# A sequence in the Mamba stage as two blocks of 128 steps, with a state handed from the first to the second

## The chip, the cores and the metric

The kernel runs on one core of a Trainium2 chip. The metric is the device time of one launch in microseconds (us). The time before is the median of three runs.

## What is computed

The reference is a chain of four residual layers over 4096 tokens of 128 features (16 sequences of 256 steps), each ahead of it a layer norm: a latent attention, six layers of local attention with a feed-forward, a Mamba layer (state-space scan), and two more layers of local attention with a feed-forward. The change touches only the Mamba layer. Its core in the reference, cut to what matters (four heads of 64 channels, a state of 64):

```python
X = x * dt[..., None]
Adt = A * dt
...
A_cumsum = jnp.cumsum(Ac, axis=-1)
Lmat = jnp.exp(segsum(Ac))                       # exp(sum of A*dt over j < k <= i), 0 above the diagonal
Y_diag = jnp.einsum('bclhn,bcshn,bhcls,bcshp->bclhp', Cc, Bc, Lmat, Xc)
decay_states = jnp.exp(A_cumsum[..., -1:] - A_cumsum)
states = jnp.einsum('bclhn,bhcl,bclhp->bchpn', Bc, decay_states, Xc)
...
state_decay_out = jnp.exp(A_cumsum)
Y_off = jnp.einsum('bclhn,bchpn,bhcl->bclhp', Cc, states, state_decay_out)
Y = (Y_diag + Y_off).reshape(b, L, NHEADS, HEADDIM) + x * D[:, None]
y = Y.reshape(b, L, D_INNER)
y = y * jax.nn.silu(z)
y = y * jax.lax.rsqrt(jnp.mean(y * y, axis=-1, keepdims=True) + EPS) * norm_w
return jnp.einsum('bld,ed->ble', y, out_proj_w)
```

The length of the chunks is free: any split of the sequence gives the same result, as long as the state at a chunk's start carries what came earlier. Each sequence starts from `init_states`.

## The kernel before

Activations are kept with the 128 features on the partitions. Between the layers, x lies in DRAM (`xd`), 512 tokens (two sequences) to a tile, eight tiles in all. The Mamba stage (`mamba`) has two kinds of work, written as generators that are advanced in turn; here no order is written out by hand, a scheduler orders the instructions of each engine from what they depend on and from its own costs. The attention layers before and after it do have an order by hand (`PLAN32`, `PLAN64`) and are not touched.

`project(t)` takes a tile of 512 tokens: `normed` (center on TensorE at L149, mean of squares at L157, `var` on VectorE at L161, `rstd` as a power on GpSimd at L116, its spread over the partitions at L167), then the step sizes `dt` and `a` = A*dt (L1375, `softplus`), the convolution's three groups of channels (L1385 with four VectorE taps each, L1388 and L1393, and a Silu on ScalarE) and the gate `sz` (L1411).

`scan(b)` takes one sequence of 256 steps. It uses PSUM pools of two banks each (`s`, `mm`, `o`; `t` is the projection's):

- `pc` (pool `s`): C times B for the pairs of steps, blocks (0,0), (0,1) and (1,1) of 128x128, 384 columns; `cbm` on VectorE multiplies by the triangle `tri` of three blocks.
- `xdt`: x turned by four transposes (L1451), times dt.
- For each of two groups c of two heads: `ab` copies on GpSimd, running sums of `a` by matmuls with `tri` (L1469, L1470), their exp `ce` times C (L1473). For each head: weights `w0`, `w1` on VectorE (L1479, L1480), three matmuls for the segment sums of the three blocks (L1482, L1483, L1486), exp on ScalarE (L1488), product with `cbm` on GpSimd (L1489). Then `py` (pool `o`): the initial state times `ce` (L1493), and for each head and block of earlier steps a matmul of 64 columns (L1497).
- `y2`: plus D*x (L1504), times the gate (L1507), squares `sq` on GpSimd (L1509), their mean (L1515), `var` (L1519), `rstd` (L116), its spread (L1525), the scaling (L1530), the output projection (L1533), and the addition to x (L1534).

`leave(t)` stores the tile and norms it once more for the next attention layers (`norm_to_y`, whose two VectorE products are L180). Two sequences are in flight at a time, and the next tile's projection and the last tile's `leave` are advanced between their steps. On SP the stage issues eight loads (L1351) and eight stores (L1538, L1580).

TensorE's f32 matmul appears in the trace as two passes, so its counts are twice the calls; transposes have one.

Of the kernel before, what the change touches and what calls it, by code (L numbers as in the profile page):

```python
# [22 lines left out]
F32 = mybir.dt.float32  # L23
BF16 = mybir.dt.bfloat16
I32 = mybir.dt.int32
AF = mybir.ActivationFunctionType
ALU = mybir.AluOpType
AX = mybir.AxisListType

P = 128  # L30
B = 16
S = 256
# [1269 lines left out]
def mamba(ctx: ExitStack, k: Stack, m: Scan, last, later):  # L1302
# [9 lines left out]

    nc = k.nc
    H, DI, NC = 4, 256, 3
    TAPS = 4
# [1 line left out]
    work = ctx.enter_context(k.tc.tile_pool(name="mb_work", bufs=2))  # L1319
    deep = ctx.enter_context(k.tc.tile_pool(name="mb_deep", bufs=4))  # L1320


    tri = once.tile([P, 3, P], F32, name="tri")
    nc.gpsimd.memset(tri, 1.0)
    for i in (0, 2):
        nc.gpsimd.affine_select(
            out=tri[:, i, :],
            in_=tri[:, i, :],
            compare_op=ALU.is_ge,
            fill=0.0,  # L1330
            base=0,
            pattern=[[1, P]],
            channel_multiplier=-1,
        )
    tri = tri.rearrange("p c l -> p (c l)")
    gt = once.tile([P, P], F32, name="gt")
    nc.gpsimd.memset(gt, 1.0)
    nc.gpsimd.affine_select(
# [1 line left out]
    )  # L1340
    mean_w = once.tile([P, 1], F32, name="mb_mean_w")
    nc.gpsimd.memset(mean_w, 1.0 / DI)

    xs = {}

# [88 lines left out]
    def scan(b):  # L1434
# [3 lines left out]
        sl = slice(i0 * S, (i0 + 1) * S)  # L1438
        toks = [slice(i0 * S + i * P, i0 * S + (i + 1) * P) for i in range(2)]

        pc = k.ps("s")
        nc.tensor.matmul(pc[:, 0:S], bT[:, toks[0]], cT[0:E, sl], start=True, stop=True)
        nc.tensor.matmul(pc[:, S : 3 * P], bT[:, toks[1]], cT[0:E, toks[1]], start=True, stop=True)
        cbm = work.tile([P, 3 * P], F32, tag="cbm", name=k.name("cbm"))
        nc.vector.tensor_mul(cbm, tri, pc[:, 0 : 3 * P])
        xdt = work.tile([P, 2, H, E], F32, tag="xdt", name=k.name("xdt"))
        pt = k.ps("mm")
        for i in range(2):
# [5 lines left out]
            pt.rearrange("p (i h e) -> p i h e", i=2, e=E),  # L1454
            dt[:, 2 * i0 : 2 * i0 + 2, :].unsqueeze(3).to_broadcast([P, 2, H, E]),
        )
        yield
        y2 = work.tile([P, 2, S], F32, tag="y2", name=k.name("y2"))
        sqs = []
        for c in range(2):  # L1460
            pcs = k.ps("mm")[:, 0:S]
            sums = []
            for i in range(2):
                ab = deep.tile([P, 2, E], F32, tag=f"ab{i}", name=k.name("ab"))
                nc.gpsimd.tensor_copy(
                    ab, a[:, 2 * i0 + i, 2 * c : 2 * c + 2].unsqueeze(2).to_broadcast([P, 2, E])
                )
                sums.append(ab.rearrange("p h e -> p (h e)"))
            nc.tensor.matmul(pcs, sums[0], tri[:, 0:S], start=True, stop=False)  # L1469
            nc.tensor.matmul(pcs[:, P:S], sums[1], tri[:, 0:P], start=False, stop=True)  # L1470
            ce = work.tile([P, S], F32, tag="ce", name=k.name("ce"))
            nc.scalar.activation(ce, pcs, AF.Exp)
            nc.gpsimd.tensor_mul(ce, ce, cT[:, sl])  # L1473
            gs = []
            for h in (2 * c, 2 * c + 1):
                a0, a1 = (a[:, 2 * i0 + j, h : h + 1] for j in range(2))
                w0 = deep.tile([P, P], F32, tag="w0", name=k.name("w0"))
                w1 = deep.tile([P, P], F32, tag="w1", name=k.name("w1"))
                nc.vector.tensor_scalar_mul(w0, gt, a0)  # L1479
                nc.vector.tensor_scalar_mul(w1, gt, a1)  # L1480
                pseg = k.ps("s")
                nc.tensor.matmul(pseg[:, 0:S], w0, tri[:, 0:S], start=True, stop=False)  # L1482
                nc.tensor.matmul(  # L1483
                    pseg[:, P:S], a1.to_broadcast([P, P]), tri[:, 0:P], start=False, stop=True
                )
                nc.tensor.matmul(pseg[:, S : 3 * P], w1, tri[:, 0:P], start=True, stop=True)  # L1486
                g = deep.tile([P, 3 * P], F32, tag="g", name=k.name("g"))
                nc.scalar.activation(g, pseg[:, 0 : 3 * P], AF.Exp)  # L1488
                nc.gpsimd.tensor_mul(g, g, cbm)  # L1489
                gs.append(g)  # L1490
                yield
            py = k.ps("o")[:, 0:S]
            nc.tensor.matmul(py, initT[:, c, :], ce, start=True, stop=False)  # L1493
            for j in range(2):
                for i in range(2):
                    rows = slice(64 * i, 64 * i + 64)
                    nc.tensor.matmul(  # L1497
                        py[rows, j * P : S],
                        xdt[:, j, 2 * c + i, :],
                        gs[i][:, j * S : S + j * P],  # L1500
                        start=False,
                        stop=(j == 1),
                    )
            nc.vector.scalar_tensor_tensor(  # L1504
                y2[:, c, :], xc[:, c, sl], dcol[:, c : c + 1], py, ALU.mult, ALU.add
            )
            nc.vector.tensor_mul(y2[:, c, :], y2[:, c, :], sz[:, c, sl])  # L1507
            sq = deep.tile([P, S], F32, tag="sq", name=k.name("sq"))
            nc.gpsimd.tensor_mul(sq, y2[:, c, :], y2[:, c, :])  # L1509
            sqs.append(sq)  # L1510
            yield
# [162 lines left out]
```

## Time and profile before

| | us |
|---|---|
| median of 3 runs (4847.5 to 4858.25) | 4850.86 |
| the profiled execution, its own time | 4845.01 |
| its span | 4843.3 |
| Mamba stage in it, from its first memset (L1324) to its last addition's end (L1534) | 3745.7 to 4079.3 |
| one pair of sequences in that stage | 37.1 |

The page lists per engine the busy share of 40 equal slices of the span, a row with the granted TensorE clock in tenths, the chain of work that ended last, and groups of instructions by line with their count, busy time, mean and the idle time before them. A group's idle time names what ended it. Windows give the same busy times for a stretch between two times. A line can be that of a helper: L149 to L180 are called from `project` and from `leave`.

### The profile page before, as it was taken

The page shows a single profiled execution, that of the slowest core. Times are in us where ns is not written, and L with a number is a line of the kernel's source. Part 1 is how long each engine was busy: PE and PEld are TensorE (multiplying, and loading weights), DVE is VectorE, ACT ScalarE, POOL GpSimd, SP SyncE. Part 2 cuts the span into 40 slices and gives each one's busy share as a digit, 9 for nine tenths or more (in the row PEclk, how much of TensorE's full clock was granted, in tenths as well). Part 3 has the DMA queues.
Part 4 walks back from the last instruction along what each step waited for, and adds up shares of the span by engine and source line. Part 5 has one row for each costly group of instructions (what it writes and reads, how often), then busy time and mean ns, then how long its engine had stood idle before and what let it go on. Part 6 is the DMA issues. An engine that isn't in the chain of part 4 may idle for free.

```text
span 4843.3 us, 121149 instructions
## 1 busy us (share of the span) xinstructions
PE 4570.3 (94%) x50834; PEld 3051.0 (63%) x50834; DVE 3371.2 (70%) x4050; ACT 2745.0 (57%) x3412; POOL 3297.2 (68%) x3603
## 2 busy tenths in 40 slices
PE   7986899999999999999999999999998898999998
PEld 4553566666666666666666666666665665566664
DVE  4664777777777777777777777777773675788775
ACT  2553465666656666566655666556664453565554
POOL 2434677777777777777777777777774344777774
PEclk9998999999999999999999999999999898999999
DMA  1111010000100010001000010000011000111111
GB/s 32 36 32 45 16 39 16 16 16 18 39 16 21 16 41 16 16 16 39 17 16 16 16 39 17 16 16 23 23 26 30 25 12 18 55 45 44 49 57 39
DMA packets 208040, 131.52 MB, mean 27 GB/s; under 512 B 61261, under 2 KB 179417, under 8 KB 207497
## 3 DMA queue, kind: packets, MB, share of 16 engines
q1 hardware_dynamic: 197096, 118.78, 9.9%
q8 instruction: 403, 6.60, 0.6%
q0 software_dynamic: 8704, 4.48, 0.5%
q14 instruction: 141, 1.15, 0.1%
q10 hardware_dynamic: 1696, 0.51, 0.0%
HBM read 29.65 MB, written 8.39 MB: 8 GB/s over the span
## 4 chain that ended last, share of the span: by engine, by line
PE 71%; DVE 16%; POOL 5%; ACT 4%; issue 2%; SPq 1%; DMA 0%; DVEq 0%; ACTq 0%; POOLq 0%
PE py L1107 13%; PE pq L792 7%; PE hid L1164 6%; PE u L1081 6%; PE pk L792 5%; PE scores L994 5%; PE tq L882 4%; DVE n L849 3%; PE tp L1040 3%; PE fy L1198 3%; PE tk L882 2%; DVE rotq L817 2%; PE st L383 2%; POOL rstd L116 1%; DVE rotk L817 1%
## 5 line engine op out<-in xcount | busy, mean ns | idle before, releaser
L1107 PE MATMUL py<-oT,wvo 128*128 128x256 f32 x3072 | 679.0, 379 | 1.2 <-ACT oT L1094 1.2
L1034 POOL TENSOR_TENSOR pr<-pr,rs 128x1024 f32<-128x1024 f32 x256 | 489.5, 1912 | 275.5 <-DVE rs L1029 234.1
L853 POOL TENSOR_TENSOR rotq<-rotq,t2q 128x1024 f32<-128x1024 f32 x256 | 605.0, 2363 | 36.3 <-DMA w<-in_L_ffn_W 23.8
L1107 PEld LDWEIGHTS py<-oT,wvo 128*128 128x128 f32 x3072 | 576.4, 190 | 75.8 <-ACT oT L1094 1.6
L1094 ACT COPY oT<-u 128x1024 f32<-128x1024 f32 x384 | 377.0, 1015 | 316.0 <-PE u L1081 307.7
L792 PE MATMUL pq<-wqkv,y 128*128 128x512 f32 x1024 | 493.2, 605 | 25.8 <-DMA wqkv<-in_L_ffn_Wqkv 14.1
L873 POOL TENSOR_TENSOR rotq<-rotq,rn 128x1024 f32<-128x1024 f32 x256 | 488.9, 1910 | 11.2
L101 DVE TENSOR_TENSOR y<-y,py 64x256 f32<-64x256 f32 x256 | 107.2, 419 | 525.1 <-PE py L1107 523.4
L817 DVE TENSOR_TENSOR rotq<-pq,tab 128x1024 f32<-128x1024 f32 x256 | 313.3, 1224 | 220.6 <-ACT sqq L803 150.2
L899 ACT COPY qT<-tq 128x1024 f32<-128x1024 f32 (+1 forms) x256 | 230.7, 901 | 412.1 <-PE tq L882 412.1
L853 POOL TENSOR_TENSOR rotk<-rotk,t2k 128x1024 f32<-128x1024 f32 x192 | 453.9, 2364 | 0.0
L994 PEld LDWEIGHTS scores<-kT,qT 64*32 64x32 f32 (+1 forms) x26624 | 322.0, 108 | 160.2 <-issue 97.2
L1025 DVE TENSOR_REDUCE rs<-pr 128x16 f32<-128x1024 f32 (+1 forms) x256 | 312.3, 1220 | 156.7 <-ACT pr L1018 152.0
L803 ACT ACTIVATE sqq<-pq 128x1024 f32<-128x1024 f32 x256 | 261.9, 1023 | 263.3 <-PE pq L792 245.4
L1081 PE MATMUL u<-prT,vc 64*128 64x256 f32 x3072 | 404.4, 394 | 2.1 <-DVE t2k L829 0.3
L994 PE MATMUL scores<-kT,qT 64*32 64x64 f32 (+2 forms) x26624 | 400.6, 225 | 4.7 <-ACT kT L899 2.8
L792 PE MATMUL pk<-wqkv,y 128*128 128x512 f32 x768 | 393.4, 601 | 0.0
L1164 PE MATMUL hid<-fxn,w 128*128 128x512 f32 (+1 forms) x768 | 387.1, 615 | 4.8 <-DVE ga L1186 2.7
L862 POOL TENSOR_SCALAR rn<-n 128x64 int32<-128x64 int32 (+1 forms) x128 | 30.3, 236 | 518.7 <-DVE n L849 518.7
L873 POOL TENSOR_TENSOR rotk<-rotk,rn 128x1024 f32<-128x1024 f32 x192 | 365.3, 1903 | 0.1
L1018 ACT ACTIVATE pr<-pr 128x1024 f32<-128x1024 f32 x256 | 270.6, 1057 | 134.9 <-DVE pr L1010 125.2
L1005 DVE TENSOR_REDUCE nm<-scores 128x16 f32<-128x1024 f32 (+1 forms) x256 | 311.5, 1217 | 21.9 <-PE scores L994 21.0
(285 smaller groups left out, 9773.1 us busy)
## 6 DMA issues: line engine op xcount, KB each, us to landing
vc<-vt SPq DMA_DIRECT2D x1152, 32.0 KB
vc<-vt SPq DMA_DIRECT2D x64, 256.0 KB
vc<-vt SPq DMA_DIRECT2D x96, 128.0 KB
vc<-vt SPq DMA_DIRECT2D x576, 16.0 KB
wqkv<-in_L_ffn_Wqkv SPq DMA_DIRECT2D x12, 512.0 KB
x<-xd SPq DMA_DIRECT2D x23, 256.0 KB
xd<-x SPq DMA_DIRECT2D x22, 256.0 KB
wo<-in_L_ffn_Wo SPq DMA_DIRECT2D x6, 512.0 KB
```

The costliest lines, as they stand in the source:

```text
L792: self.nc.tensor.matmul(pq[:, 512 * int(half) : 512 * int(half) + 512], self.k.y[:, b, c0 : c0 + P], L.wqkv[:, col : col + 512], start=Tru ...
L817: self.nc.vector.tensor_mul(rot.rearrange("p (w h) e -> p w h e", w=ways), self.get(n, "p" + group).rearrange("p (w h e) -> p w h e", w=wa ...
L853: self.nc.gpsimd.tensor_add(rot, rot, self.done(n, "t2" + group))
L873: self.nc.gpsimd.tensor_mul(rot, rot, rn.unsqueeze(2).to_broadcast(list(rot.shape)))
L994: self.nc.tensor.matmul(sc[ch * W : (ch + 1) * W, par, c, first : self.KS], qT[rows, c, ch * W : (ch + 1) * W], kT[rows, c, t0 - W + first ...
L1005: self.nc.vector.tensor_reduce(nm, self.get(n, "scores"), AX.X, ALU.max, negate=True)
L1025: self.nc.vector.tensor_reduce(rs, self.by_head(n), AX.X, ALU.add)
L1034: self.nc.gpsimd.tensor_mul(pr, pr, rs)
L1081: self.nc.tensor.matmul(pu[:, par, :, j, :], self.vc[n % 3][rows, ch, :], prT[rows, :, ch * W : (ch + 1) * W], start=True, stop=True,)
L1094: self.nc.scalar.copy(self.get(n - blk, "oT")[:, :, q0 : q0 + 64].rearrange("p (c i) q -> p i c q", i=2), self.done(n, "u" + half).rearran ...
L1107: self.nc.tensor.matmul(py, w[:, c, :], oT[:, c, :], start=(c == 0), stop=(c == last))
L1164: self.nc.tensor.matmul(pg[0:n, at : at + TT], L.w1[:, col : col + n], self.get(t, "fxn"), start=True, stop=True,)
```

## The change

A sequence becomes two blocks of 128 steps. Inside a block everything is as before; the block (0,1), which joined early steps with late ones, is gone, and in its place the state at the end of the first block is formed and used for the second. In detail:

- `tri` is one triangle of 128x128, not three blocks.
- `pc` holds two blocks of C times B, and beside them B turned for the first block (L1451 of the new file) and the sum of `a` from each step to the block's end (L1452); ScalarE copies the first to `bs` and takes the exp of the second, `ea`; GpSimd forms `xa`, the first block's `xdt` times `ea` (L1475).
- The running sums restart in the second block, two matmuls of 128 columns (L1486). Their exp is kept as `decay`, for the state's update, beside `ce`.
- Segment sums of both heads and both blocks: one VectorE product for the weights (`seg`, L1499), four matmuls of 128 columns into one bank (L1510), one exp (L1514) and one product (L1515) of 512 columns.
- The state: two matmuls of 64x64 into a bank of pool `o` (L1521), each followed on VectorE by the initial state times the block's decay plus that product (L1524). Four state tiles take turns; they are zeroed once.
- The output: for each block the state at its start times `ce` (L1536), then the two heads' matmuls (L1538).

L1545, L1548, L1550, L1556, L1560, L1566, L1571, L1574 and L1575 of the new file are L1504, L1507, L1509, L1515, L1519, L1525, L1530, L1533 and L1534 of the old one.

```diff
-    tri = once.tile([P, 3, P], F32, name="tri")
+    tri = once.tile([P, P], F32, name="tri")
...
+    states = [once.tile([P, P], F32, name=f"state{i}") for i in range(4)]
+    for state in states:
+        nc.gpsimd.memset(state, 0.0)
...
         pc = k.ps("s")
-        nc.tensor.matmul(pc[:, 0:S], bT[:, toks[0]], cT[0:E, sl], start=True, stop=True)
-        nc.tensor.matmul(pc[:, S : 3 * P], bT[:, toks[1]], cT[0:E, toks[1]], start=True, stop=True)
-        cbm = work.tile([P, 3 * P], F32, tag="cbm", name=k.name("cbm"))
-        nc.vector.tensor_mul(cbm, tri, pc[:, 0 : 3 * P])
+        for i in range(2):
+            nc.tensor.matmul(
+                pc[:, bass.ts(i, P)], bT[:, toks[i]], cT[0:E, toks[i]], start=True, stop=True
+            )
+        nc.tensor.transpose(pc[:, S : S + E], bT[:, toks[0]], k.ident[0:E, 0:E])
+        nc.tensor.matmul(pc[:, S + E : S + E + H], gt, a[:, 2 * i0, :], start=True, stop=True)
+        cbm = work.tile([P, 2, P], F32, tag="cbm", name=k.name("cbm"))
...
+        bs = work.tile([P, E], F32, tag="bs", name=k.name("bs"))
+        nc.scalar.copy(bs, pc[:, S : S + E])
+        ea = work.tile([P, H], F32, tag="ea", name=k.name("ea"))
+        nc.scalar.activation(ea, pc[:, S + E : S + E + H], AF.Exp)
...
+        xa = work.tile([P, H, E], F32, tag="xa", name=k.name("xa"))
+        nc.gpsimd.tensor_mul(xa, xdt[:, 0], ea.unsqueeze(2).to_broadcast([P, H, E]))
...
-            nc.tensor.matmul(pcs, sums[0], tri[:, 0:S], start=True, stop=False)
-            nc.tensor.matmul(pcs[:, P:S], sums[1], tri[:, 0:P], start=False, stop=True)
+                nc.tensor.matmul(
+                    pcs[:, bass.ts(i, P)],
+                    ab.rearrange("p h e -> p (h e)"),
+                    tri,
+                    start=True,
+                    stop=True,
+                )
+            decay = work.tile([P, S], F32, tag="decay", name=k.name("decay"))
+            nc.scalar.activation(decay, pcs, AF.Exp)
             ce = work.tile([P, S], F32, tag="ce", name=k.name("ce"))
-            nc.scalar.activation(ce, pcs, AF.Exp)
-            nc.gpsimd.tensor_mul(ce, ce, cT[:, sl])
...
-                nc.vector.tensor_scalar_mul(w0, gt, a0)
-                nc.vector.tensor_scalar_mul(w1, gt, a1)
-                pseg = k.ps("s")
-                nc.tensor.matmul(pseg[:, 0:S], w0, tri[:, 0:S], start=True, stop=False)
+            nc.gpsimd.tensor_mul(ce, decay, cT[:, sl])
+            seg = deep.tile([P, 2, 2, P], F32, tag="w", name=k.name("w"))
+            nc.vector.tensor_mul(
+                seg,
+                gt.unsqueeze(1).unsqueeze(1).to_broadcast([P, 2, 2, P]),
...
+            pseg = k.ps("s")
+            for h in range(2):
+                for i in range(2):
+                    nc.tensor.matmul(
+                        pseg[:, bass.ts(2 * h + i, P)], seg[:, h, i], tri, start=True, stop=True
+                    )
+            g = deep.tile([P, 2, 2, P], F32, tag="g", name=k.name("g"))
+            nc.scalar.activation(g.rearrange("p h i l -> p (h i l)"), pseg, AF.Exp)
+            nc.gpsimd.tensor_mul(g, g, cbm.unsqueeze(1).to_broadcast([P, 2, 2, P]))
+            yield
+            pst = k.ps("o")
+            state = states[(2 * b + c) % 4]
+            for h in range(2):
+                rows = slice(64 * h, 64 * h + 64)
                 nc.tensor.matmul(
-                    pseg[:, P:S], a1.to_broadcast([P, P]), tri[:, 0:P], start=False, stop=True
+                    pst[rows, 64 * h : 64 * h + 64], bs, xa[:, 2 * c + h], start=True, stop=True
                 )
-                nc.tensor.matmul(pseg[:, S : 3 * P], w1, tri[:, 0:P], start=True, stop=True)
-                g = deep.tile([P, 3 * P], F32, tag="g", name=k.name("g"))
...
+                nc.vector.scalar_tensor_tensor(
+                    state[rows, rows],
+                    initT[rows, c, rows],
+                    decay[rows, P - 1 : P],
+                    pst[rows, rows],
+                    ALU.mult,
+                    ALU.add,
+                )
+            yield
             py = k.ps("o")[:, 0:S]
-            nc.tensor.matmul(py, initT[:, c, :], ce, start=True, stop=False)
-            for j in range(2):
-                for i in range(2):
-                    rows = slice(64 * i, 64 * i + 64)
+            for i, of in enumerate((initT[:, c, :], state)):
+                cols = bass.ts(i, P)
+                nc.tensor.matmul(py[:, cols], of, ce[:, cols], start=True, stop=False)
+                for h in range(2):
                     nc.tensor.matmul(
...
```

## The prediction

> **What bounds the kernel now.** I read the slices of the page first, to find the stage that the change touches, then windows of that stage, its groups by form, its chain of waits, and the timeline of TensorE.
>
> ```profile
> PE   7986899999999999999999999999998898999998
> ...
> PEclk9998999999999999999999999999999898999999
> ```
>
> The Mamba stage lies in slices 31 to 34: its first memset (L1324) starts at 3745.7 us, its last addition (L1534) at 4078.9. Everything the diff edits lies there, 333 us or 6.9% of the span, so no edit can move the total by more than a few per cent. Windows, first of the stage before and then of one pair of sequences in Mamba:
>
> ```profile
> 3550.00:3600.00 50.00, 49.30 (x620) 35.32 (x619) 35.09 (x38) 28.33 (x32) 36.54 (x43) 1.00 0.11 27
> ...
> 3861.40:3898.50 37.10, 34.26 (x195) 25.19 (x194) 26.34 (x72) 21.24 (x31) 18.95 (x28) 0.95 0.05 15
> 3898.50:3935.70 37.20, 34.71 (x195) 25.34 (x194) 26.63 (x73) 21.22 (x31) 18.94 (x28) 0.95 0.05 15
> ```
>
> Columns: length, then busy PE, PEld, DVE, ACT, POOL, then the granted clock. A pair of sequences repeats every 37.1 us. TensorE is busy for 34.5 of them, VectorE 26.5, ScalarE 21.2, GpSimd 18.9; the clock is 0.95, where the earlier stage has 1.00. So TensorE leads, but not alone: something makes it pause and lose clock. The chain of waits shows the pause, once per pair (start, length, what):
>
> ```profile
> 3912.26 0.57 PE o L1497 x2
> 3912.83 0.63 PE mm L1469 x2
> ...
> 3914.94 0.17 DVE var L161
> ...
> 3915.18 1.02 POOL rstd L116
> ...
> 3919.51 0.86 POOL sq L1509
> ...
> 3921.52 0.70 POOL rstd L116
> ...
> 3922.94 0.85 PE mm L1469 x2
> ```
>
> For 28 us of each 37 the chain is TensorE alone; then two norm chains (mean on PE, var on DVE, rstd on POOL, spread on PE) come out from behind it. On TensorE's timeline they are three gaps, 2.49 us together:
>
> ```profile
> 3916.24 0.65 PE L167 MATMUL t<-ident,rstd 128*128 128x128 f32 x4 [0.67 <-POOL rstd L116]
> ...
> 3920.41 0.83 PE L1515 MATMUL o<-mb_mean_w,sq 128*128 128x1 f32 x6 [0.79 <-POOL sq L1509]
> 3922.27 0.67 PE L1525 MATMUL mm<-ident,rstd 128*128 128x128 f32 x2 [1.03 <-POOL rstd L116]
> ```
>
> The groups that change, by form:
>
> ```profile
> L1489 POOL TENSOR_TENSOR g<-g,cbm 128x384 f32<-128x384 f32 x64 | 63.8, 996 | 27.2 <-ACT g L1488 27.2
> L1482 PE MATMUL s<-tri,w 128*128 128x256 f32 x128 | 40.9, 402 | 0.0
> L1488 ACT ACTIVATE g<-s 128x384 f32<-128x384 f32 x64 | 30.7, 490 | 75.4 <-PE s L1486 65.2 <-POOL sq L1509 10.1
> ```
>
> The matmul means contain pipeline latency, so I price TensorE by the spacing of its pieces in the chain. An f32 matmul is two passes: 128 columns cost 0.22 us, 256 cost 0.43, 512 cost 0.86; one to four columns against full weights cost 0.20 (L1515, four matmuls in 0.79); a 128-column transpose 0.11.
>
> **TensorE's work, per pair of sequences.** Each sequence has two groups (c), so four groups per pair.
> Running sums: 0.43 + 0.22 become two of 0.22, -0.21 per group. Segment sums: two heads of 0.43 + 0.22 + 0.22 become four of 0.22, 1.74 to 0.88, -0.86.
> The output matmuls and the new state matmuls use half the array (64 columns), and there the trace shows a price for each change of shape: L1497 x2 takes 0.57 for 0.43 of columns (0.14 on entry), and the full-array L1469 after it 0.63 for 0.43 (0.20 on exit), 0.34 per block. The two heads overlap inside a block: L1497 x8 takes 0.80 where its columns add to 1.30. The old output group is 0.43 + 0.80 + 0.20 = 1.43. The new one has two blocks, because each time block puts a full-array matmul (L1536) ahead of its two heads: 2 x (0.22 + 0.14 + 0.22 + 0.20) = 1.56, +0.13.
> The state matmuls (L1521, 64 columns, 0.11) are eight per pair. In the built order five stand alone among full-array matmuls (0.45 each) and three beside another small block (0.15, from 0.11 up to 0.2): 2.7 per pair, 0.68 per group.
> Per group -0.26, per pair -1.0. The bank with C times B gains a transpose and a 4-column matmul and loses a quarter of its columns: 0.99 to 1.09 per sequence, +0.2. Sum: **-0.8 us per pair**, out of 32.4.
>
> Here a rule of the Trainium skill speaks against the change: TensorEngine Tiling (Array Packing), Key Properties, says that changing the tiling mode drains the engine. It names no price. By columns alone (no drain) the same list gives -1.04 per group and -4.0 per pair; by the row (0.34 per block, and the pair goes from 6 such blocks to 18) it is -0.8. I take the row.
>
> **The other engines.** VectorE: 16 weight scalings (0.302 and 0.347, 5.2 us) become four of 128x512 (0.68, as L1452 with its broadcast); cbm shrinks by 0.1 twice; eight state updates of 64x64 come in, bounded by 0.23 (L1429, 16 elements) and 0.30 (L1479, 128), at 0.25: -0.7 per pair. ScalarE: eight exps of 0.49 become four of about 0.60 (L1412's 128x512 takes 0.589), and two copies and two exps of some 0.2 (L1422) come in: -0.7; the table loads (1.283 each) stay eight per pair in the built order. GpSimd: eight products of 0.996 become four of 1.3 (by elements; 0.96 if half of L1034), and xa costs 0.70 twice (between L1509 and L1473): -1.4. None of the three is the bound, with 10 to 18 us free per pair, so these gains count as nothing: TensorE's 32 us hide them. The DMAs (L1351, L1538, L1580) keep number and order on SP. Four new memsets on POOL (0.20 each, as L1337), less one select and a shorter tri, come while POOL is 5.3 us ahead of its next need at 3759: nothing. If that cover were gone, 0.3 us.
>
> **The waits.** TensorE takes its instructions in order, so I laid the built order of the changed kernel beside these durations. Four places decide, the same in five consecutive pairs:
> 1. L157 is followed at once by L167. Between them lies var, rstd and hand-overs: 3914.91 to 3916.24, 1.33 us, uncovered. Before, matmuls between them left 0.67.
> 2. From L167 to the squares' mean (now L1556): two L180 (0.69 each), one product (0.35), sq (about 0.7), hand-overs, 2.65 us. Only L149 (0.86) covers it now: 1.8, before 0.79.
> 3. The mean to L1566: 1.03 as before.
> 4. New: the next tile's rstd on POOL has been queued behind ce, xa and sq, and that ce waits for decay, which needs L1486, placed after L157. From L1486: decay 0.4, ce 0.73, xa 0.70, sq 0.62, rstd 1.02, hand-overs 0.25, 3.7 us. TensorE has L1510 x4, one L1536 and one L1538 meanwhile (1.46), then stands at L167: 2.25. In the trace of before this L167 starts without a gap. Behind it on TensorE wait the other half of the output, the next state and the projections.
> Idle time 2.49 becomes 6.4: **+3.9 us per pair**.
> L1521's second half waits for L1524 on VectorE, since both halves of a state share one bank tile. In the order other matmuls stand between, and I find VectorE there in time: bounded by 0 and, if VectorE is in the middle of a 0.74 us tap each time, about 0.4 four times; I take 0.
>
> **The clock.** After the 2.49 us of gaps within 7 us, L1469 takes 0.85 for 0.43 and four L1533 passes 1.67 for 0.87: about 1.7 us lost per pair. The skill's TensorE: Matmul & The Clock Gate (Why this matters for your kernels) warns of idle gaps above some 3 us; by that, no gap here or in the new order would cost clock. The row shows that several short ones do. A lone 2.25 us gap is between: 0 by the rule, 1.7 by the row. I take 1.2, nearer the row: **+1.2**.
>
> **The sum.** -0.8 + 3.9 + 1.2 = +4.3 per pair, five pairs, +21.5. The last pair has places 1 to 3 without L149 as cover: +1.7. The first, -0.8; the tail, where the state hand-over has nothing beside it, +0.5 (0 to 3). Total +23 on the profiled run's 4845.0 (span 4843.3 and 1.7 around it). The median shown is 4850.9, 5.9 above that execution, so against the median I expect 4874.
>
> **The rivals.**
> (a) It is faster: the work removed is real (a quarter of the time steps' products on every engine), drains overlap with weight loads, and the lighter VectorE and GpSimd reach their norm chains sooner. It decides where TensorE saves more than the gaps grow: with -4.0 per pair and gaps up by 2, it is -2 over eight pairs, 4835. For it: every engine's busy time falls. Against it: the entry and exit prices in the trace, and gap 4, which hangs on order, not load.
> (b) Saving and waits cancel: gap 4 half covered, no second clock loss, cheap states: +0.8 per pair, 4855.
> (c) The waits of L1521 and of the two "o" banks (twelve uses per pair instead of eight) really bite: another 1.6 to 3 us per pair, 4886.
> That the change does not do what it says is excluded by the built order: the segment sums stand there as four 128-column matmuls per two heads.
>
> **The numbers.** Main case 0.52, (a) 0.18, (b) 0.15, (c) 0.15. Main case alone: gaps half as bad and no second clock loss give 4858, a cold clock of twice the length there 4885. The range 4843 to 4892 leaves out most of (a) and the end of (c). A difference under 0.2%, 9.7 us, is about what a measurement of this kernel can't tell from none. Faster by more: (a), 0.18. Within: (b) and the main case's low end, 0.17. Slower: 0.65.
>
> **What would show it.** Right: pairs 40 to 43 us apart, a gap above 2 us at L167 behind POOL's rstd with ce, xa, sq before it, clock under 0.95, L1521 with an L1510 or L1468 after it that takes 0.1 to 0.2 more. Wrong: pairs under 37 us, or no gap at the second L167, or L1521 blocks without entry and exit cost. A stage longer with TensorE's gaps elsewhere (at L1521 or L1536, released by VectorE) would be (c).

## The result, and the profile after

The changed kernel takes 4926.53 us (median of 5, 4921.13 to 4942.42) against 4854.69 for the kernel before (median of 5): ratio 1.0155, 95% interval 1.0143 to 1.0166. It is slower, as forecast, but by 72 us instead of 23, outside the range. The profiled execution took 4926.89 us, 81.9 more than that of before: the Mamba stage grew from 333.6 to 406.4 us (+72.8); it also began 7.5 us later, ahead of anything the change touches (stage starts of 3744 to 3764 us occur in the runs below), and 1.6 came after it. So below I compare the stage and its pairs (a pair: two sequences, the unit that repeats).

The page's slices of the changed kernel, TensorE's busy share and granted clock:

```profile
PE   7896899999999999999999999999997888899998
...
PEclk9998999999999999999999999999997767999999
```

Slices 31 to 34 hold Mamba. Before, the clock row read 9, 8, 9, 8 there; now it reads 7, 7, 6, 7, while TensorE's busy share reads 7, 8, 8, 8 (before 8, 8, 9, 8): it is at work, at about half speed for much of the time. Windows of the changed kernel, one pair of sequences each (length; busy PE, PEld, DVE, ACT, POOL; granted clock; DMA):

```profile
3853.46:3899.23 45.77, 40.21 (x210) 28.65 (x209) 27.25 (x70) 20.94 (x33) 17.77 (x26) 0.81 0.04 12
3899.23:3947.13 47.90, 43.14 (x211) 30.28 (x210) 27.18 (x70) 20.61 (x32) 17.78 (x26) 0.71 0.04 11
3947.13:3997.75 50.62, 45.96 (x209) 32.00 (x208) 26.32 (x71) 20.17 (x31) 17.80 (x26) 0.66 0.04 11
3997.75:4051.84 54.09, 49.05 (x209) 34.32 (x208) 26.43 (x70) 20.61 (x32) 17.83 (x26) 0.62 0.01 5
4051.84:4097.51 45.67, 39.96 (x211) 28.60 (x210) 27.27 (x71) 20.95 (x33) 17.78 (x26) 0.81 0.02 6
```

The pairs are 45.7 to 54.1 us apart (before 37.1 on the mean of five) and no two are alike, though their instructions are. VectorE, ScalarE and GpSimd are busy about as long in each. What varies with the length is TensorE's busy time, 40 to 49 us, and the clock, 0.81 to 0.62. TensorE's idle time is about the same in all, 4.7 to 5.7. The idle places of the last of these pairs, from TensorE's timeline:

```profile
4058.26 0.65 PE L167 MATMUL t<-ident,rstd 128*128 128x128 f32 x4 [1.34 <-POOL rstd L116]
...
4061.84 0.83 PE L1556 MATMUL o<-mb_mean_w,sq 128*128 128x1 f32 x6 [2.07 <-POOL sq L1550]
4064.08 0.69 PE L1566 MATMUL mm<-ident,rstd 128*128 128x128 f32 x2 [1.41 <-POOL rstd L116]
...
4081.34 0.32 PE L167 MATMUL t<-ident,rstd 128*128 128x128 f32 x1 [0.87 <-POOL rstd L116]
```

These are the prediction's four places. What follows them is not what it said. The same stretch, in windows of 3.41 us (from 140 us on, every change of the granted clock in these traces falls on a grid of that step, to within 0.01 us; I call a window on it a slot):

```profile
4056.27:4059.69 3.42, 2.08 (x12) 1.25 (x12) 1.82 (x4) 3.36 (x7) 1.78 (x2) 1.00 0.00 0
4059.69:4063.10 3.41, 0.91 (x7) 0.74 (x6) 2.93 (x7) 0.99 (x3) 1.00 (x2) 1.00 0.00 0
4063.10:4066.51 3.41, 2.43 (x9) 1.87 (x10) 1.72 (x5) 0.09 (x1) 3.09 (x5) 0.50 0.00 0
4066.51:4069.93 3.42, 3.42 (x10) 2.03 (x10) 0.68 (x2) 0.77 (x2) 1.24 (x2) 0.50 0.00 0
4069.93:4073.34 3.41, 3.41 (x15) 2.26 (x14) 1.44 (x3) 0.29 (x2) 0.00 (x0) 0.50 0.00 0
4073.34:4076.75 3.41, 3.41 (x18) 2.72 (x17) 1.58 (x4) 0.00 (x0) 0.00 (x0) 0.50 0.00 0
4076.75:4080.17 3.42, 3.42 (x15) 3.20 (x16) 0.27 (x1) 0.91 (x2) 1.71 (x3) 0.50 0.00 0
4080.17:4083.58 3.41, 2.54 (x18) 1.65 (x18) 0.97 (x2) 0.07 (x1) 2.35 (x3) 1.00 0.02 5
```

The clock is either 1.00 or 0.50, for whole slots. It falls after the slot with gaps in it (0.91 us busy) and stays at half for five slots, 17 us, in four of which TensorE is busy without a pause (3.41 or 3.42 of the slot). In the pair of 54.1 us it stays for twelve slots, 41 us. In the kernel before, at the same place, it came back after one:

```profile
3993.99:3997.41 3.42, 1.60 (x10) 1.20 (x10) 1.23 (x4) 1.23 (x3) 2.06 (x3) 1.00 0.00 0
3997.41:4000.82 3.41, 3.41 (x10) 2.46 (x9) 1.29 (x3) 0.86 (x2) 3.24 (x6) 0.50 0.01 2
4000.82:4004.23 3.41, 3.41 (x25) 2.61 (x24) 1.75 (x5) 0.49 (x1) 1.05 (x2) 1.00 0.02 5
```

Added over the stage, TensorE is at half clock for 64.9 us before and 229.6 us after. Half of the difference, if TensorE leads throughout, is 82 us: more than the whole growth of the stage.

### The profile page after: what moved, and what is told of

It reads as the page before. It is cut to its first block, busy times and chain, and to the rows that moved or that the text cites. A ratio compares the mean times of both kernels' runs of the same rounds, so it can differ in the third digit from the quotient of the medians.

```text
span 4925.2 us, 121297 instructions
## 1 busy us (share of the span) xinstructions
PE 4638.0 (94%) x50946; PEld 3096.0 (63%) x50946; DVE 3371.2 (68%) x4018; ACT 2745.3 (56%) x3416; POOL 3294.8 (67%) x3590
## 4 chain that ended last, share of the span: by engine, by line
PE 72%; DVE 15%; POOL 5%; ACT 4%; issue 2%; SPq 1%; DMA 0%; DVEq 0%; ACTq 0%; POOLq 0%
PE py L1107 13%; PE pq L792 7%; PE hid L1164 6%; PE u L1081 6%; PE pk L792 5%; PE scores L994 5%; PE tq L882 4%; PE tp L1040 3%; DVE n L849 3%; PE fy L1198 3%; PE tk L882 2%; DVE rotq L817 2%; PE st L383 2%; POOL rstd L116 1%; PE scores L976 1%
## 5 line engine op out<-in xcount | busy, mean ns | idle before, releaser
L116 POOL TENSOR_TENSOR rstd<-var,neg_half 128x4 f32<-128x4 f32 (+1 forms) x112 | 113.1, 1009 | 326.9 <-DVE var L161 184.7
```

## The experiments

Two questions stood at the start: do the gaps alone set the clock, or does what TensorE does between them matter; and which part of the change brings it. "Half clock" in this table is the time at 0.50 within the stage, from the trace's record of the clock. Pairs are the last four of the five, from windows as above; a pair's bounds are one VectorE instruction that can move, so single pairs of e7 and e10 to e13 are uneven. All times are us. The kernel before differs by 4.6 us between the five calls, so medians of different rows are compared only roughly. The scheduler orders TensorE's instructions anew for every edit; where that matters, it is said.

| kernel | median, before's in the same call | ratio (95%) | stage | half clock | pairs |
|---|---|---|---|---|---|
| before | | | 333.6 | 64.9 | 37.3-37.5 |
| after | 4926.53, 4854.69 | 1.0155 (1.0143-1.0166) | 406.4 | 229.6 | 45.7-54.1 |
| e1 fill gaps | 4864.87, 4851.22 | 1.0023 (1.0016-1.0031) | 342.2 | 30.0 | 38.9 |
| e2 full state | 4879.17, 4851.22 | 1.0050 (1.0033-1.0066) | 355.7 | 148.5 | 40.0-45.2 |
| e3 no hand-over | 4849.51, 4851.22 | 0.9997 (0.9987-1.0006) | 331.3 | 114.8 | 36.0-40.7 |
| e4 before, slow norms | 4878.28, 4851.22 | 1.0056 (1.0038-1.0074) | 361.4 | 79.7 | 41.0-41.5 |
| e5 one-column fill | 4957.88, 4851.13 | 1.0225 (1.0205-1.0245) | 436.4 | 233.2 | 46.9-57.4 |
| e6 place 4 | 4876.94, 4851.13 | 1.0059 (1.0042-1.0075) | 362.2 | 148.2 | 40.7-41.7 |
| e7 full state, less fill | 4848.09, 4851.13 | 0.9995 (0.9984-1.0005) | 328.9 | 54.4 | 31.8-45.3 |
| e8 before, fill | 4845.78, 4851.13 | 0.9990 (0.9982-0.9999) | 330.0 | 34.9 | 37.7 |
| e9 quarter fill | 4892.35, 4850.06 | 1.0077 (1.0058-1.0095) | 372.1 | 77.1 | 40.8, one 48.3 |
| e10 full state, place 4 | 4872.20, 4850.06 | 1.0046 (1.0029-1.0062) | 350.3 | 123.5 | 39.0-42.8 |
| e11 e7 with a third fill | 4859.45, 4850.06 | 1.0020 (1.0012-1.0027) | 340.5 | 75.4 | 31.0-41.3 |
| e12 full state, ce, late fill | 4849.55, 4851.11 | 0.9999 (0.9990-1.0009) | 327.5 | 51.8 | 35.0-38.6 |
| e13 after, late fill | 4894.52, 4851.11 | 1.0088 (1.0069-1.0107) | 381.7 | 112.6 | 42.3-49.7 |
| e14 before, late fill | 4846.57, 4851.11 | 0.9994 (0.9985-1.0003) | 327.0 | 31.2 | 37.2-37.3 |

**e1: fill the gaps with matmuls.**

```diff
+        for _ in range(2):                       # ahead of the spread L167
+            nc.tensor.matmul(ps[:, 0:S], self.center, x[:, 0:S], start=True, stop=True)
...
+        for _ in range(3):                       # ahead of the squares' mean L1556
+            nc.tensor.matmul(ps[:, P : P + S], k.center, xc[:, 0, sl], start=True, stop=True)
...
+        for _ in range(2):                       # ahead of the spread L1566
+            nc.tensor.matmul(pb[:, 0:S], k.center, xc[:, 0, sl], start=True, stop=True)
```

> The changed kernel with matmuls whose result is overwritten (128x256, 0.43 us each at full clock) put on TensorE ahead of the four waits for a norm: two before each spread L167, three before the squares' mean L1556, two before the spread L1566. They cost nothing while TensorE would stand anyway. Theory 1 (the idle gaps alone bring TensorE to half clock and keep it there for 17 to 40 us): the gaps fall below 0.6 us, the granted clock of a pair returns to 0.95 or more, pairs go from 45-54 us to 39-42, the time from 4926 to 4870-4885. Theory 2 (the mix of half-array matmuls, short transposes and drains looks like little work to the clock, the gaps only start it): the clock of a pair stays at 0.8 or below and the time at 4910-4930. Theory 3 (waits between L1521 and its update on VectorE, the 'o' banks): nothing changes but the gaps, 4905 or more.

The windows of two steady pairs:

```profile
3911.94:3950.86 38.92, 38.92 (x238) 28.78 (x237) 26.73 (x70) 18.05 (x29) 18.32 (x27) 1.00 0.04 15
3950.86:3989.78 38.92, 38.92 (x238) 28.79 (x237) 26.73 (x70) 18.06 (x29) 18.32 (x27) 1.00 0.02 7
```

Six microseconds of useless work per pair (14 x 0.43) shorten a pair by 7 to 15 us. TensorE never stands and the clock is 1.00, with all half-array blocks still there. So those blocks do not bring the clock down by themselves, and the real work of a pair at full clock is 38.92 - 6.0 = 32.9 us, a little less than the kernel before's (34.85 busy less 1.7 of half clock, 33.2). Theory 3 (waits at L1521) is out: they would have stayed. Not all of it is the filling: the order changed too, and a 512-column matmul now stands between the mean and its spread (L1562 and L1574 here), where the changed kernel stands idle for 1.41 us:

```profile
3923.88 0.95 PE L1562 MATMUL o<-mb_mean_w,sq 128*128 128x1 f32 x8
3924.69 1.11 PE L1572 MATMUL mm<-xc,center 128*128 128x256 f32 x4
3925.64 1.02 PE L150 MATMUL t<-x,center 128*128 128x512 f32 x2
```

**e5: the same filling with hardly any columns.** This separates "busy" from "columns".

```diff
-        for _ in range(3):
-            nc.tensor.matmul(ps[:, P : P + S], k.center, xc[:, 0, sl], start=True, stop=True)
+        for _ in range(6):                       # likewise 4 for 2 at the other places
+            nc.tensor.matmul(ps[:, P : P + 1], k.center, xc[:, 0, 0:1], start=True, stop=True)
```

> As e1_fill_gaps, at the same places, but each added 128x256 matmul (0.43 us) is replaced by two of a single column (about 0.2 us each, like those of L1556): TensorE is as busy as in e1 at the four waits, and hardly any columns pass through its array. Theory W (the clock is set every 3.41 us by the columns that passed in that stretch, weighted by the share of the array used: below some 0.36 of what full clock could pass it is halved, and at half clock it comes back only above some 0.73 of what half clock can pass): several stretches per pair have 0.10 to 0.35 without the added columns, so the clock falls as in the changed kernel, 0.6-0.85 per pair, and the time is 4890-4935. Theory G (idle time decides): no gap, clock 1.00, pairs of 38.9, 4865.

It is slower than the change itself. Windows on the 3.41 us grid:

```profile
4058.54:4061.96 3.42, 3.42 (x20) 2.21 (x19) 3.40 (x12) 3.38 (x4) 0.73 (x3) 1.00 0.00 0
4061.96:4065.37 3.41, 3.41 (x24) 2.00 (x22) 2.78 (x6) 3.36 (x6) 2.16 (x7) 1.00 0.20 77
4065.37:4068.78 3.41, 3.41 (x33) 3.41 (x32) 0.30 (x2) 3.35 (x6) 0.90 (x2) 1.00 0.00 0
4068.78:4072.20 3.42, 3.42 (x11) 2.28 (x12) 1.45 (x3) 0.14 (x1) 0.94 (x1) 0.50 0.00 0
```

TensorE is busy without a pause in three slots, and the clock is halved after the third: its 33 passes are nearly all of one column. So TensorE's idle time is not all that the clock goes by. (The order of e5 is not e1's, so the difference of their times is not the columns' alone; this slot is.)

From this I worked out, for each slot in all sixteen traces (from 3800 us to the stage's end), the share of it that passing columns fill: each pass of TensorE taken singly, and 128 columns counted as the 0.107 us (0.213 at half clock) that such passes are apart in the timelines. Of 1111 slots at full clock, 122 were followed by half clock; of 315 at half clock, 109 by full. A limit of 0.38 at full clock and 0.78 at half sorts all but 19 and 31 of them. Sorted by TensorE's busy time, the best limits leave 58 and 97 wrong, the second hardly better than saying "never comes back" (109). At 1.00 a column takes half as long, so both limits are about the same number of columns per slot. In the slots of the changed kernel shown above the shares are 0.38, 0.00 (falls), then at half clock 0.50, 0.65, 0.76, 0.47, 0.91 (comes back); in the kernel before 0.16 (falls), then 1.06 (comes back). In the last slot of e5 above at full clock it is 0.01. The limits are fitted to these slots; e9 below sharpens them.

**e2 and e3: what keeps it at half.** e2 makes the two half-array state products one:

```diff
-        bs = work.tile([P, E], F32, tag="bs", name=k.name("bs"))
-        nc.scalar.copy(bs, pc[:, S : S + E])
+        bs = work.tile([P, 2, E], F32, tag="bs", name=k.name("bs"))
+        nc.scalar.copy(bs, pc[:, S : S + E].unsqueeze(1).to_broadcast([P, 2, E]))
...
-                nc.tensor.matmul(pst[rows, 64 * h : 64 * h + 64], bs, xa[:, 2 * c + h], ...)
+            nc.tensor.matmul(pst[:, 0:P], bs.rearrange(...), xa[:, 2 * c : 2 * c + 2].rearrange(...), ...)
```

> The changed kernel with the state products L1521 as one full-array matmul per group (B twice side by side, 128 rows, both heads' 128 columns, the two diagonal blocks used) in place of two half-array ones: eight half-array matmuls of 18 blocks per pair go, and with them the wait of the second for the first's update on VectorE. Theory 1 (gaps set the clock): TensorE's work falls by about 1.9 us per pair (2.7 to 0.9 at full clock), the gaps stay, the clock of a pair stays at 0.62-0.81: 4905-4915. Theory 2 (the half-array blocks keep the clock low): the half-clock stretch is cut by half, clock about 0.88: 4880-4890. Theory 3 (waits at L1521): what they cost goes too, more than 2 us per pair with no change of the clock.

```profile
3933.78:3978.00 44.22, 39.05 (x203) 28.96 (x202) 27.88 (x70) 20.70 (x32) 17.45 (x26) 0.77 0.04 13
3978.00:4021.93 43.93, 38.97 (x203) 29.03 (x202) 27.87 (x71) 20.61 (x32) 17.45 (x26) 0.77 0.02 6
```

47 us come back, where 1.9 us per pair of TensorE's work would give 15. The gaps are still there (1.34, 1.75, 1.41 at the first three places in the pair at 3978): the difference is that half clock now mostly lasts 13.7 to 20.5 us after them, not 17 to 41. A state product that stands alone between full-array matmuls takes 0.35 to 0.41 us at full clock in the trace of the changed kernel, for 0.11 of columns. That eight fewer leave the slots fuller is the likely reason for the shorter stretches; the half-clock slots up to 4055 us fill 0.66 with columns on the mean, against 0.63.

e3 leaves the state out (with the lines shown go `bs`, `ea`, `xa`, the state products and their updates; part of the computation is not done):

```diff
-        nc.tensor.transpose(pc[:, S : S + E], bT[:, toks[0]], k.ident[0:E, 0:E])
-        nc.tensor.matmul(pc[:, S + E : S + E + H], gt, a[:, 2 * i0, :], start=True, stop=True)
...
-            for i, of in enumerate((initT[:, c, :], state)):
+            for i, of in enumerate((initT[:, c, :], initT[:, c, :])):
```

> The changed kernel without the hand-over: the second block of 128 steps starts from the initial state as the first does, so the transpose of B, the sums to the block's end, their exp and copy, xa, the state products and their updates are left out (part of the computation is not done). What remains is the smaller segment sums, two heads in a bank, and the two output blocks. Theory 1: TensorE has about 3.2 us less per pair, xa's 0.57 goes from the queue before the second rstd, the other gaps stay, so the clock stays below 0.9: 4890-4905. Theory 2: only 8 half-array blocks per pair as against 6 in the kernel before, so the clock is back at 0.93 or more: 4850-4860. The blocks and banks by themselves gain, and all the loss is the hand-over: below 4845.

The time is that of the kernel before (ratio 0.9997), so the smaller sums and shared banks by themselves neither gain nor lose, and the loss comes only with the hand-over. The longer waits are there without it: TensorE stands 4.9 to 6.0 us in a pair (2.5 before). Its busy time is 30.0 to 35.6 us per pair at a clock of 0.79 to 0.95: what the blocks save in columns also takes columns out of the slots, and part of the gain goes into half clock (114.8 us against 64.9).

**e4: the gaps in the old mix.**

```diff
-        self.nc.gpsimd.tensor_tensor(out, in_, self.neg_half[:, : in_.shape[1]], ALU.pow)
+        for _ in range(2 if self.fill else 1):   # set inside Mamba alone
+            self.nc.gpsimd.tensor_tensor(out, in_, self.neg_half[:, : in_.shape[1]], ALU.pow)
```

> The kernel before with the pow of every norm inside Mamba done twice on GpSimd (1.02 us more between each variance and its spread), nothing else: gaps like those of the changed kernel in a stream of matmuls with the old mix. Per pair of sequences four norms; the gaps at L167 go from 0.67 and 0 to 1.7 and up to 1.0, the one at L1525 from 1.03 to 2.05, twice in a pair or once where it is covered: 3 to 4 us of idle time per pair. Theory 1: the clock of a pair falls from 0.95 to 0.62-0.85 and pairs go from 37 to 45-52 us: 4910-4960. Theory 2: idle time alone, and about 1 us of clock: pairs of 41, 4880-4890.

```profile
3878.74:3920.20 41.46, 36.37 (x196) 26.03 (x195) 26.70 (x74) 21.45 (x32) 22.26 (x32) 0.92 0.04 13
3920.20:3961.55 41.35, 36.26 (x196) 26.24 (x195) 26.71 (x74) 21.47 (x32) 22.25 (x32) 0.92 0.05 14
```

Idle time is 5.1 us per pair, the same as in the changed kernel, though its gaps (1.76, 1.80, 1.07 and 0.46 us in one pair) stand further apart. A pair is 41.4. Nearly every fall lasts one slot of 3.41 us: with the 256 and 512 column matmuls of the old mix, columns fill 0.97 of these slots on the mean, against 0.63 in the changed kernel. This is what the prediction had in mind: +2.6 of idle and +1.7 of clock. The changed kernel has as much idle time and a thinner stream behind it.

**e6 and e10: the queue on GpSimd (place 4).**

```diff
-            nc.gpsimd.tensor_mul(ce, decay, cT[:, sl])
+            nc.vector.tensor_mul(ce, decay, cT[:, sl])
...
-        nc.gpsimd.tensor_mul(xa, xdt[:, 0], ea.unsqueeze(2).to_broadcast([P, H, E]))
+        nc.vector.tensor_mul(xa, xdt[:, 0], ea.unsqueeze(2).to_broadcast([P, H, E]))
```

> The changed kernel with the products ce (128x256) and xa (128x4x64) on VectorE in place of GpSimd, so that the next tile's rstd is no longer queued behind them. The step of the prediction (place 4 costs 2.25 us and 1.2 us of clock per pair): the gap at the second L167 goes below 0.3, five pairs each shorter by 2 to 3.5: 4909-4916. Theory W: the other three gaps still halve the clock, and the mix keeps it there; a place of 0.7-0.9 in half clock goes, nothing else: 4915-4926, clock of a pair below 0.85. VectorE (27 us of a pair) would be too late with y2 for L1556: slower than 4926.

Both expectations were too small: nearly 50 us came back. Idle places of two pairs in a row (of the first, the last two):

```profile
3974.52 0.65 PE L167 MATMUL t<-ident,rstd 128*128 128x128 f32 x4 [1.03 <-POOL rstd L116]
3978.43 0.83 PE L1556 MATMUL o<-mb_mean_w,sq 128*128 128x1 f32 x6 [2.40 <-POOL sq L1550]
...
4012.14 0.49 PE L1536 MATMUL o<-ce,state 128*128 128x128 f32 x2 [0.16 <-DVE state L1524]
4015.91 0.65 PE L167 MATMUL t<-ident,rstd 128*128 128x128 f32 x4 [1.71 <-POOL rstd L116]
4018.56 1.22 PE L1448 MATMUL s<-cT,bT 64*128 64x128 f32 x4 [0.53 <-DVE cT L1411]
```

Not only the fourth gap went but that at L1566 too, and in some pairs that at L1556 (in others it is 1.55 to 2.40 us): the scheduler gave TensorE another order, so this run does not price place 4 alone. Idle time per pair is 2.4 to 4.2 us, half clock 10 to 17 us.

e10 is e2's and e6's edits together. 

> The full-array state product of e2 and ce and xa on VectorE as in e6, no filling. e2 took 47 us off, e6 50. If the two work on different terms (fewer half-array blocks end a half-clock stretch sooner, shorter gaps start fewer) both count: clock of a pair 0.90 or more, 4845-4860. If each only does what the other has already done, and the gap of 1.4 us at L167 is left as the trigger: one stretch per pair of 10 us, clock 0.85-0.88, 4865-4876.

 The two overlap: 123.5 us at half clock against 148.5 and 148.2, and a time that cannot be told from e6's (the intervals of the ratios overlap). The gap at L167, 0.95 to 1.23 us, is still there, with shorter ones near it.

**e7, e11, e12: towards a faster version.** e7 has e2's and e6's edits and fills 1, 2 and 1; e11 1, 3 and 1; e12 e2's edit, only `ce` on VectorE, and fills of 1, 2 and 2 that read what was made just before the wait:

```diff
-            nc.tensor.matmul(ps[:, P : P + S], k.center, xc[:, 0, sl], start=True, stop=True)
+            nc.tensor.matmul(ps[:, P : P + S], k.center, y2[:, 1, :], start=True, stop=True)
```

> The full-array state product of e2, ce and xa on VectorE as in e6, and a smaller filling: one 128x256 matmul before each L167, two before L1556, one before L1566 (eight per pair, 3.4 us at full clock; e1 had fourteen, 6.0). e1 at full clock shows 38.9 - 6.0 = 32.9 us of real work per pair, less 1.9 for the states. Theory W: clock 0.97 or more in a pair, pairs 34.5-36.5, time 4832-4845, below the kernel before. If the smaller filling leaves a stretch below the threshold, that pair gets one or more half-clock stretches of 3.41 us (1.7 us each, longer if the mix holds it down): pairs 38-41, 4855-4875.

> e7_full_state_less_fill with a third matmul before the squares' mean (1, 3, 1 at L167, L1556, L1566). In e7 the clock fell only in stretches of 0.29 and 0.31 of the columns (two of 6.8 us in the steady pairs), each with the squares' mean in it; 0.43 us of columns more makes 0.41 of them. Expected: no half-clock stretch in the steady pairs, clock 1.00, the 3.4 us lost in each fall come back, at most 0.86 us per pair of added work on the path: 4838-4846, just below the kernel before. If the added work lies on the path everywhere: 4846-4852, the same as e7.

> Full-array state product, ce (not xa) on VectorE, and filling matmuls that read the result made just before the wait (y before the squares' mean, the squares before L1566's spread and before L167's), so that they stand inside the gap and not several us ahead of it as in e7 and e11: one at each L167, two at L1556, two at L1566 (ten per pair, 4.3 us). Theory W: no stretch of a steady pair below 0.36, clock 1.00; real work 31.0 + 4.3 of filling, of which the gaps of 3 to 5 us hide most: pairs of 34.5-36, 4830-4842, faster than the kernel before. If the phase of the stretches still meets the few-column means and a gap together: one fall in some pairs, 4845-4858.

Windows of e7:

```profile
3874.79:3906.58 31.79, 29.13 (x188) 22.08 (x189) 24.39 (x69) 16.74 (x27) 12.04 (x19) 1.00 0.03 9
3906.58:3951.85 45.27, 43.34 (x246) 31.94 (x244) 33.23 (x84) 25.46 (x38) 15.19 (x21) 0.92 0.05 18
```

e7 keeps full clock between its first pair and its end except in two falls of 6.8 us, and equals the kernel before (0.9995). e11 was meant to remove those two and is slower: one more matmul gave another order, in which the filling was over 1.7 us before the gap began (at 3923.86 TensorE has waited 1.20 us for `sq`), and the clock fell in four places. e12 puts them inside the gaps: one fall of 3.4 us in five pairs, stage 327.5 against 333.6, and a time of 4849.55 (0.9999): the filling seems to take what the clock gives. No version is clearly faster than the kernel before.

**e8 and e14: the kernel before with its clock kept up** (one fill ahead of each of L1515 and L1525, in e14 reading y2 and the squares).

> The kernel before with one 128x256 matmul, whose result is overwritten, ahead of the squares' mean L1515 and one ahead of the spread L1525 (four per sequence pair, 1.7 us at full clock, part of it in the 2.5 us of gaps). Theory W: the stretch of each pair that has 0.14-0.19 of the columns gets 0.25 more, stays above 0.36, and the one half-clock stretch per pair (3.41 us, 1.7 us lost) goes: clock 1.00, pairs from 37.3 to 35.7, 4835-4846. Idle time decides and 1.0 us gaps remain: clock 0.95, pairs of 37.4-38.5, 4852-4860.

> The kernel before with one filling matmul that reads y ahead of L1515 and one that reads the squares ahead of L1525 (e8 with the filling inside the gaps). e8 had clock 1.00 and pairs still of 37.7, since its added 1.7 us stood elsewhere on TensorE. Inside the gaps of 2.5 us they cost little: pairs of 35.7-36.5 and 4836-4844 if the 1.7 us of half clock per pair is on the path; 4846-4852 if the wait of the next norm takes its place.

Both have clock 1.00 in the steady pairs and pairs of 37.2 to 37.7, as long as before: the added 1.7 us replace the 1.7 us lost at half clock. e8 is lowest of all, 0.9990 (0.9982 to 0.9999), too small a difference to build on.

**e9: does the share of the array count?** e1's filling with `k.center[0:E, 0:E]`, 64 rows by 64 columns of weights.

> As e1_fill_gaps, with as many added matmuls of 256 columns at the same places, but each with 64 rows and 64 output columns of the array instead of 128 and 128. The columns that pass and the time on TensorE are those of e1 (and some 0.34 us more per block for the change of shape). If columns alone count (or time busy), no stretch is below the threshold: clock 1.00, pairs of 39-40.5, 4865-4880. If the share of the array counts (a quarter here), the stretches of e1 with 0.10-0.34 from the other matmuls come to 0.21-0.35: one or two falls to half clock per pair, and the mix holds it there: clock of a pair 0.65-0.85, 4890-4930.

```profile
3928.08:3968.85 40.77, 40.77 (x237) 26.62 (x236) 26.74 (x71) 18.17 (x29) 18.40 (x27) 1.00 0.04 14
3968.85:4017.18 48.33, 48.33 (x237) 30.69 (x236) 26.34 (x70) 18.16 (x29) 18.37 (x27) 0.82 0.02 6
```

The matmuls of the steady pairs stand in e1's order, and as many columns pass. Yet one of the four steady pairs falls to half clock, where none did in e1; the 1.85 us that the others are longer go with the change of shape. The slots of this run tell more. The slot ahead of that fall is filled 0.51 by columns, while others with 0.49 stayed; and at half clock two slots filled 0.95 were followed by another at half, while 0.80, 0.82 and 0.83 brought full clock back. Counted by columns, the best limits for this run leave 4 of 82 and 4 of 12 slots wrong. With each pass weighted by the share of the array that its weights take (64 x 64 is a quarter), they leave 0 and 1. Over all sixteen traces, limits of 0.34 and 0.75 on the weighted share leave 14 and 9 wrong instead of 19 and 31. So in this stage the share of the array counts too; whether by its rows, its columns or both, these runs do not tell. The limits are this stage's: between 140 and 600 us of the same traces, where other matmuls run, they leave 32 of 1739 and 74 of 402 slots wrong.

**e13: late filling in the changed kernel.**

> The changed kernel with nothing altered but ten filling matmuls per pair that stand inside the gaps (one at each L167, two at L1556, two at L1566). If the clock alone made the change slower (e1: 32.9 us of real work per pair at full clock, against 33.2 in the kernel before), the steady pairs are at clock 1.00 and 37.0-38.5, 4850-4862: no difference from the kernel before beyond 0.25%. If the longer gaps cost by themselves as much as the prediction said (3.9 us per pair), pairs of 39.5-41 at clock 1.00: 4866-4880.

Neither: the filling now waits for y itself (L1552 on VectorE, 1.37 or 1.65 us in a pair), a gap stays, and the clock is 0.83 to 0.92. So this run does not separate the gaps' own cost from the clock's; e1 bounds it, in its own order: at full clock the same work and six microseconds of filling make 38.9 us.

## Why the prediction was wrong in size

The direction, the four places and the order of instructions were right. Per pair, against the terms of its sum:

- **Work on TensorE, -0.8.** Held: 32.9 us (e1) against 33.2 (before, less its half clock); e14 gives 33.8 for before, so -0.3 to -0.9. By columns alone it would have been -4.0; the price of entry and exit was about right, a little high (a lone state product takes 0.35 to 0.41, said 0.45).
- **Waits, +3.9.** The first three places came at 1.34, 1.2 to 2.1 and 1.41 us (said 1.33, 1.8, 1.03), the fourth at 0.69 to 0.87 (said 2.25). Idle time per pair is 5.1 on the mean of the five, 2.5 before: +2.6. TensorE is mostly at half clock ahead of place 4, and slower with what covers the wait. But the place was also sized too large: in e2's last pair it has the clock at 1.00 ahead of it and is 1.39:

```profile
4046.57 0.65 PE L167 MATMUL t<-ident,rstd 128*128 128x128 f32 x4 [1.39 <-POOL rstd L116]
```

- **Clock, +1.2.** This is the step that failed: it let each clock loss last one slot. (The two rows that it read there make 1.2 of its 1.7; the whole slot at half clock makes the 1.7.) TensorE's busy time averages 43.7 us (40.21, 43.14, 45.96, 49.05, 39.96) for 32.9 of work at full clock: 10.8 us, against 1.7 before, **+9.1**. The sum -0.3 + 2.6 + 9.1 = 11.4 meets the measured 11.7 (48.8 against 37.1 on the mean of five pairs). The split rests on e1, which has another order. Without it: TensorE is busy at half clock for 24.9 us per pair, half of which is 12.4, against 1.6 before; then the work is -1.7 and the clock +10.8. By either count the clock is the term that was mis-sized.
- **The ends.** The two windows ahead of the five pairs took 68.5 us for 56.5 (+12.0, said -0.8), by the same cause: half clock from 3810.5 to 3817.3 and from 3827.6 to 3848.1, where before had none. The last took 62.1 for 59.8 (+2.3, said +1.7 and 0.5). Five pairs 58.6, the head 12.0, the end 2.3: 72.9, the stage's growth.

Why the step failed: the trace of before shows the fall and a return one slot later, and I took that return for a property of the clock. It went with the stream behind the gap, which in the kernel before fills 0.86 to 1.06 of the half-clock slot in each pair with columns. The change thins this very stream: 128-column matmuls for 256-column ones, half-array blocks with their changes of shape, a matmul of four columns, between the norms' one-column matmuls; its half-clock slots up to 4055 us fill 0.63 on the mean, and those that brought full clock back at least 0.79. So a cost that the prediction priced once (1.7 us) is paid for 5 to 12 slots. The data were there: the windows of before on a 3.41 us grid, and the columns in the built order, give the fill of each slot.

The rule weighed there, TensorE: Matmul & The Clock Gate of the Trainium skill (Why this matters for your kernels), warns of idle gaps above some 3 us; no gap of the changed kernel's five pairs is above 2.1, and in e5 the clock fell after three slots without any. The same page (What's actually happening) does state a free-running window of 3413 ns, which the grid in these traces is, and a return after one busy window of some 3.4 us; here a window of unbroken work was not enough: 117 half-clock slots with TensorE busy throughout were followed by another.

Of the rivals, (c) is out: TensorE's idle time at L1521 and L1536 in the whole stage is 1.1 us together. (a) fails by its own condition: the gaps grew by 2.6 us per pair and TensorE saved 0.3 to 1.7, the clock aside. (b) counted on no second clock loss, and that loss is most of the result. Of the signs that the prediction named, the gap above 2 us at the second L167 did not come; the direction came out right since waits and clock both had the right sign.

## What to carry to other kernels

Where a row of granted clock shows a dip, look at it slot by slot on its 3.41 us grid, and work out what share of each slot columns fill, both in the slot with the gap and in those after it: here a change that makes matmuls smaller turned one slot at half clock into five to twelve. Price a gap by what runs behind it, not by its length alone. A full-array matmul with half of its result unused (e2) was cheaper than two half-array ones, and moving two products off the queue ahead of a norm (e6), with the new order that came with it, was worth far more than the wait it was meant to remove.

## What the runs showed of the hardware that I had not expected

- The granted clock took the values 1.00 and 0.50 alone and changed only on a grid of 3.413 us, free of the kernel's own period: five alike pairs took 45.7 to 54.1 us.
- Over sixteen traces of this stage it mostly fell after a slot with less than about 0.38 of full clock's columns, and returned after one with at least about 0.78 of half clock's; weighted by the share of the array in use, 0.34 and 0.75 sort the slots better. 21 of 122 falls came with TensorE busy throughout.
- The same filling in the same order with a quarter of the array (e9) let the clock fall in one of four steady pairs, with the full array (e1) in none.
- Six microseconds of matmuls whose result is overwritten, added to each pair (e1), took some 60 us off the changed kernel, with the other order that they brought.
